# Layers 2 and 3 of a four-layer graph network written in source order, batch by batch

## The chip, the cores and the metric

The kernel runs on one core of a Trainium2 chip. The metric is the device time of one execution in microseconds (us), lower is better. A core has five engines with a queue of instructions each: PE (TensorE, matrix products; PEld is its weight load), DVE (VectorE), ACT (ScalarE), POOL (GpSimd) and SP (SyncE, which here only issues DMAs). Each engine takes its instructions in order; they wait for one another by semaphores.

## The reference, cut to what matters

x is (32, 512, 128): 32 batches of 512 nodes with 128 features; adj is one 512 x 512 matrix for all. Each of four layers normalises x, takes the ReLU as h, and adds the layer's output to x. The change touches layers 2 and 3:

```python
def layernorm(x): return (x - mean(x)) / sqrt(var(x) + 1e-5)      # over the features
# layer 2
h = maximum(layernorm(x), 0)
features = relu(h @ psi_w + psi_b)
messages = einsum('nm,bnd->bmd', adj * adj, features)
x = x + relu(concat(messages, h) @ phi1_w + phi1_b) @ phi2_w + phi2_b
# layer 3
h = maximum(layernorm(x), 0)
A = einsum('bnd,bmd->bnm', h @ q, h @ k) / sqrt(128)
A = exp(tanh(A / 8) * 8) * adj
x = x + (A / sum(A, -1)) @ h @ v
```

## The kernel before, in words

x stays in SBUF for all 32 batches, two batches to a group q (16 groups, `xt[q]`). Nodes are split into NT = 4 tiles of 128. Products that must be exact are made from fp32 operands of four-byte kind (f32, two PE instructions each) or from three `fp32r` parts of an operand, high, low and mid, with one PE instruction for each part and tile.

Three helpers make the parts. `moving_parts` (L397 to L399): high by a copy on ACT, low by a subtraction on POOL, mid by a scalar_tensor_tensor on DVE. `scaled_parts` (L403 to L405), for an operand that is LOW = 4096 times too large: high on ACT, low on DVE, then mid = high - low on POOL, which so waits for DVE. `fixed_parts` (L409 to L412) splits a weight.

**h and its transpose.** `stats_steps` (L243 to L254) has four bn_stats instructions for a group on DVE, a square root on ACT, a reciprocal and a product on DVE. `normed` (L263) makes h by eight ReLUs on ACT. `turn_steps` (L299 to L308) turns it feature-major: a 32 x 32 block transpose on DVE for each batch, four DMAs into a buffer in DRAM (d_hT), and one DMA back (hT, four buffers that layer 1 uses too).

**Layer 2, `layer2(q)`**, a generator for each group: h, hT; features (p_feat on PE, L1067 on DVE adds the bias, ReLU L1068 on ACT, `moving_parts`); messages (`mixed_parts`, L383, 12 matmuls for a batch with the three parts of the squared adj, evicted by ACT, L385); the bias phi2b added to x on POOL (L1081); the hidden layer (L1086, L1087, ReLU L1088 on ACT); the projection (p_l, L425) and the addition to x (L1092, DVE); then statistics for layer 3.

**Layer 3, `layer3(q)`**: h, hT; key parts by `moving_parts`; the product of the keys with qk = q k^T (L1116, three matmuls), evicted by DVE as qkh (L1118, scaled by LOW), and `scaled_parts` of it as the query; hv = h v with a column of ones (L1124, L1125); scores (L1131, 12 matmuls), Tanh (L1132) and Exp (L1136) on ACT, the mask product (L1138) for two tiles on DVE and two on POOL; A v (L1148, p_av, 32 instructions), a reciprocal (L1150) and an update of x (L1153, DVE); the store of the batch.

**What sets the order.** Layers 0 and 1 stand inside `tc.manual_schedule`, in which PE, DVE, ACT and POOL get their instructions in source order. It is left (`by_source.__exit__`, L1213) before layers 2 and 3. Their generators are stepped in turn (L1214 to L1223: `layer2` of groups 0 and 1, then one generator more in each turn), and the framework's scheduler, by its own costs and what is ready, then decides the order on each engine. Layer 1 calls `more(step)` around its last group: step 0 and 1 before the four blocks of `mix` (L977, L981), steps 2 to 5 after each.

Of the kernel before, what the change touches and what calls it, by code (L numbers as in the profile page):

```python
# [29 lines left out]
def kernel(  # L30
# [69 lines left out]
    def wide_tile(name, dtype=F32):  # L100
        return after.tile([P, 4, N], dtype, tag="wide", name=name, bufs=6)
# [92 lines left out]
    nc.vector.memset(eps, EPS)  # L194
    nc.scalar.activation(prep.tile([P, 1], F32, name="powers"), eps, AF.Exp)
# [14 lines left out]
    def ln_stats(q):  # L210
        for _ in stats_steps(q):
            pass
# [24 lines left out]
    def stats_steps(q):  # L237
# [11 lines left out]
        nc.scalar.activation(sd, st[:, :, :, 2], AF.Sqrt, bias=eps, scale=1.0 / D)  # L249
# [17 lines left out]
    def normed(q):  # L267
        h = normed_tile(q)
        for _ in normed_steps(q, h):
            pass  # L270
        return h
# [16 lines left out]
    def transposed(h, name):  # L288
        done = {}
        for _ in turn_steps(h, name, done):  # L290
            pass
        return done[name]
# [101 lines left out]

    def moving_parts(x, high, low, mid):

        nc.scalar.activation(high, x, AF.Copy, scale=DOWN)  # L397
        nc.gpsimd.tensor_sub(low, x, high.bitcast(F32))  # L398
        nc.vector.scalar_tensor_tensor(mid, x, 1.0 / UP, high.bitcast(F32), OP.mult, OP.subtract)  # L399
# [7 lines left out]
    def fixed_parts(x, high, low, mid):  # L407

        nc.scalar.activation(high, x, AF.Copy, scale=DOWN)  # L409
        nc.gpsimd.tensor_sub(x, x, high.bitcast(F32))  # L410
        nc.scalar.activation(low, x, AF.Copy, scale=LOW)
        nc.gpsimd.tensor_sub(mid, high.bitcast(F32), low.bitcast(F32))  # L412
# [635 lines left out]
    msgs, values, qk_parts = [], {}, []  # L1048

    def values_tile(q, b):  # L1050

        r = q + 2 * b
        if r not in values:
            values[r] = wide_tile(f"hv_{r}")
        return values[r].rearrange("p t n -> p (t n)").rearrange("p (b n) -> p b n", b=2)[:, b]

    def layer2(q):
        h = normed(q)
        yield
        hT = transposed(h, f"hT2_{q}")  # L1060
        yield
        yield
        feat = []
        for b in range(2):
            pf = projected(f"p_feat_{q}_{b}", (at(hT, b), psi))
            feat.append(small_tile(f"feat_{q}_{b}"))
            nc.vector.tensor_add(tiles(feat[b]), pf, spread(psib, NT))  # L1067
            nc.scalar.activation(feat[b], feat[b], AF.Relu)  # L1068
        right = [three(f"feat_{q}_{b}") for b in range(2)]
        for b in range(2):  # L1070
            moving_parts(feat[b], *right[b])
        yield
        if q % 2 == 0:
            msgs.append(wide_tile(f"msgT_{q}"))
        msgT = msgs[-1][:, 2 * (q % 2) : 2 * (q % 2) + 2]
        for b in range(2):
            mixed_parts(f"msgT_{q}_{b}", sq, right[b], msgT[:, b])
        for b in range(2):
            for i in range(0, NT, 2):
                xi = xt[q][:, b, i : i + 2, :]  # L1080
                tc.keep_in_program_order(nc.gpsimd.tensor_add(xi, xi, spread(phi2b, 2)))  # L1081
        yield
        h1T = msgT
        for b in range(2):
            ph = bank(f"p_phi1_{q}_{b}")
            nc.tensor.matmul(ph, phi1[:, 1, :], hT[:, :, b, :], start=True, stop=False)  # L1086
            nc.tensor.matmul(ph, phi1[:, 0, :], msgT[:, b], start=False, stop=True)  # L1087
            nc.scalar.activation(crossed(h1T[:, b]), split(ph), AF.Relu, bias=phi1b)  # L1088
        yield
        for b in range(2):  # L1090
            po = projected(f"p_l2_{q}_{b}", (columns(h1T[:, b]), phi2))
            nc.vector.tensor_add(xt[q][:, b], po, xt[q][:, b])  # L1092
        ln_stats(q)

    def layer3(q):
        h = normed(q)
        yield
        hT = transposed(h, f"hT3_{q}")
        yield
        keys = {}  # L1100

        def key_parts(b):
            both = wide_tile(f"key_{q}_{b}", F32R)
            keys[b] = [both[:, i].rearrange("p (t n) -> p t n", t=NQR) for i in range(3)]
            moving_parts(hT[:, :, b, :], *keys[b])

        if not qk_parts:
            parts = small_tile("qk_parts", F32R).rearrange("p (i f) -> p i f", f=D)
            qk_parts.extend(parts[:, i, :] for i in range(3))
            fixed_parts(qk, *qk_parts)  # L1110
        key_parts(0)
        yield
        for b in range(2):
            pp = bank(f"p_qkh_{q}_{b}")
            for i in range(3):
                nc.tensor.matmul(pp, qk_parts[i], keys[b][i], start=(i == 0), stop=(i == 2))  # L1116
            qkh = small_tile(f"qkh_{q}_{b}")
            nc.vector.tensor_scalar(crossed(qkh), split(pp), UP * LOW, None, OP.mult)  # L1118
            query = three(f"query_{q}_{b}")
            scaled_parts(qkh, *query)  # L1120

            pv = projected(f"p_hv_{q}_{b}", (at(hT, b), vw))
            hv = values_tile(q, b)[:, : NT * (D + 1)].rearrange("p (t f) -> p t f", f=D + 1)
            nc.vector.memset(hv[:, :, D : D + 1], 1.0)  # L1124
            nc.vector.tensor_copy(hv[:, :, :D], pv)  # L1125
            yield
            ex = wide_tile(f"ex_{q}_{b}")
            for t in range(NT):
                ps = bank(f"p_score_{q}_{b}_{t}")
                for i in range(3):  # L1130
                    nc.tensor.matmul(ps, keys[b][i][:, t, :], query[i], start=(i == 0), stop=(i == 2))  # L1131
                nc.scalar.activation(ex[:, t, :], ps, AF.Tanh, scale=UP / (8.0 * math.sqrt(D)))  # L1132
            if b == 0:
                key_parts(1)
            for t in range(NT):
                nc.scalar.activation(ex[:, t, :], ex[:, t, :], AF.Exp, scale=8.0)  # L1136
                eng = nc.gpsimd if t % 2 and q + b > 0 else nc.vector
                eng.tensor_mul(split(ex[:, t, :]), split(ex[:, t, :]), crossed(adjTx[0][:, t, :]))  # L1138
            yield
            out_r = out[2 * q + b].rearrange("(t p) f -> p t f", p=P)  # L1140
            rsum = stats.tile([P, NT], F32, tag="rsum", name=f"rsum_{q}_{b}", bufs=4)
            final = b == 1 and q == NQ - 1
            n = 1 if final else 2
            for i0 in range(0, NT, n):
                po = bank(f"p_av_{q}_{b}_{i0}").rearrange("p (i f) -> p i f", i=2)[:, :n]
                for i in range(n):
                    for t in range(NT):
                        nc.tensor.matmul(po[:, i, : D + 1], ex[:, t, blk(i0 + i)], hv[:, t, :],  # L1148
                                         start=(t == 0), stop=(t == NT - 1))
                nc.vector.reciprocal(rsum[:, i0 : i0 + n], po[:, :, D])  # L1150
                for i in range(n):
                    xi = xt[q][:, b, i0 + i, :]
                    nc.vector.scalar_tensor_tensor(xi, po[:, i, :D], rsum[:, i0 + i : i0 + i + 1], xi,  # L1153
                                                   OP.mult, OP.add)
                if final:
                    nc.sync.dma_start(out_r[:, i0, :], xt[q][:, b, i0, :])
            if not final:
                nc.sync.dma_start(out_r, xt[q][:, b])
# [22 lines left out]
    def load_mask():  # L1181

        yield
        adjTx.append(matrix_tile("adjTx"))
        load_crossed(adjTx[0], adjT_d)

    second = [layer2(q) for q in range(NQ)]
    made_square = square()

    def more(step):  # L1190

        if step in (0, 1):
            next(second[0])
        elif step == 2:
            next(second[0])
            next(second[1])
        elif step == 3:
            next(second[1])
        elif step == 5:
            ln_stats(NQ - 2)  # L1200
            ln_stats(NQ - 1)
# [10 lines left out]
    go(made_square)  # L1212
    by_source.__exit__(None, None, None)  # L1213
    waiting = [second[:2]] + [[second[q]] for q in range(2, NQ)]  # L1214
    waiting[-2].append(load_mask())
    waiting += [[layer3(q)] for q in range(NQ)]
    active = []
    while waiting or active:
        if waiting:
            active += waiting.pop(0)  # L1220
        if not waiting and len(active) == 2:
            active.reverse()
        active = [g for g in active if next(g, active) is not active]  # L1223
# [32 lines left out]
```

## Time and profile before

| what | value |
|---|---|
| median of the 3 runs shown | 936.29 us (934.6 to 937.66) |
| profiled execution, its own time | 934.17 us |
| span of it, first to last instruction | 932.1 us |
| granted PE clock over the span | 0.996 |
| first feature product of layer 2 starts | 457.5 us |
| first message product of layer 2 starts | 462.0 us |
| first score of layer 3 starts | 664.9 us |
| A v of the last batch, last start | 928.7 us |

The times of single instructions come from the profiled execution, which took 934.17 us, 2.1 us more than its span and 2.1 us less than the median of the runs. A window's row gives its length, then for each engine the busy time and the number of instructions, then the granted PE clock, the share of the DMA engines and GB/s. A group's row gives the engine, the operation, what is written and read, the number, busy time and mean of one in ns, and the idle time of its engine before it with what ended it. A row of the waits gives total us, how often, and the longest.

### The profile page before, as it was taken

What the parts mean: (1) busy time and instruction counts of PE and PEld (TensorE: products, weight loads), DVE (VectorE), ACT (ScalarE), POOL (GpSimd) and SP (SyncE); (2) the same over time, 40 slices, a digit from 0 to 9 for tenths busy, and PEclk for the clock granted to TensorE, in tenths of its full rate; (3) what the DMA queues carried; (4) which work ended last, traced back from release to release, by engine and by line L of the source; (5) the groups of instructions that cost most, each with busy time, mean ns of one, the idle gap of its engine ahead of it and who ended that gap; (6) DMA issues with size and microseconds to landing.
All of it is one profiled execution on the core that took longest, in us unless ns stands there. A gap on an engine that the chain in (4) does not pass through costs nothing.

```text
span 932.1 us, 15187 instructions
## 1 busy us (share of the span) xinstructions
PE 908.0 (97%) x5433; PEld 777.9 (83%) x5433; DVE 693.7 (74%) x1318; ACT 547.6 (59%) x1192; POOL 530.3 (57%) x461
## 2 busy tenths in 40 slices
PE   8999999999999999999899999999999999999997
PEld 4899999878888888888777777777779999999996
DVE  8888885665665655565754676767799999999995
ACT  5864552342452352353877778777767675757573
POOL 5868999742132253532135555447358787777874
PEclk9999999999999999999999999999999999999999
DMA  9256643113213312302443434343322221212111
GB/s 256 61 165 176 172 119 100 46 46 91 66 40 112 85 39 68 91 24 68 114 136 108 119 106 130 99 142 112 114 86 74 71 65 61 76 58 80 34 35 46
DMA packets 83914, 86.05 MB, mean 92 GB/s; under 512 B 6784, under 2 KB 74624, under 8 KB 83840
## 3 DMA queue, kind: packets, MB, share of 16 engines
q1 hardware_dynamic: 83552, 84.57, 31.8%
q8 instruction: 43, 0.70, 0.3%
q10 hardware_dynamic: 288, 0.52, 0.2%
q14 instruction: 31, 0.25, 0.1%
HBM read 44.17 MB, written 40.89 MB: 91 GB/s over the span
## 4 chain that ended last, share of the span: by engine, by line
PE 87%; ACT 5%; DVE 4%; POOL 2%; issue 1%; DMA 0%; POOLq 0%; ACTq 0%; DVEq 0%
PE p_av L1148 11%; PE p_l L981 10%; PE p_msgT L383 9%; PE p_score L1131 8%; PE p_x1T L383 7%; PE p_w L425 5%; PE p_l_c L371 4%; PE p_l L977 3%; PE p_l_a L371 3%; PE p_l_d L371 3%; PE p_phi L1086 3%; PE p_phi L1087 3%; PE p_g L425 3%; PE p_l L425 3%; PE p_hv L425 3%; PE p_feat L425 3%
## 5 line engine op out<-in xcount | busy, mean ns | idle before, releaser
L263 ACT ACTIVATE h<-x,sh,rs 128x128 f32<-128x128 f32 x512 | 208.2, 483 | 18.1 <-DVE sh L252 13.1
L1148 PE MATMUL p_av<-hv,ex 128*128 128x129 f32 x1024 | 122.7, 277 | 4.8 <-DVE ex L1138 3.7
L1148 PEld LDWEIGHTS p_av<-hv,ex 128*128 128x128 f32 x1024 | 120.3, 193 | 7.6 <-DVE ex L1138 4.5
L398 POOL TENSOR_TENSOR low_feat<-feat,high_feat 128x512 fp32r<-128x512 f32 x32 | 52.3, 1650 | 119.5 <-ACT high_feat L397 111.5
L1138 POOL TENSOR_TENSOR ex<-ex,adjTx 128x512 f32<-128x512 f32 x62 | 98.8, 1614 | 34.7 <-ACT ex L1136 33.5
L398 POOL TENSOR_TENSOR low_h<-h,high_h 128x512 fp32r<-128x512 f32 x32 | 48.5, 1523 | 78.6 <-ACT high_h L397 78.3
L1132 ACT ACTIVATE ex<-p_score 128x512 f32<-128x512 f32 x128 | 66.3, 612 | 44.6 <-PE p_av L1148 38.9
L385 ACT ACTIVATE x1T<-p_x1T 128x512 f32<-128x512 f32 x32 | 18.9, 592 | 124.3 <-POOL low_h L398 74.4
L243 DVE BATCH_NORM_STATS2 bn<-x 128x6 f32<-128x256 f32 x248 | 88.4, 416 | 0.2
L299 DVE STREAM_TRANSPOSE hb_hT<-h 128x512 f32<-128x512 f32 x120 | 80.1, 688 | 4.8 <-DMA d_hT<-hb_hT 2.1
L1138 DVE TENSOR_TENSOR ex<-ex,adjTx 128x512 f32<-128x512 f32 x66 | 72.3, 1101 | 13.0 <-ACT ex L1136 11.6
L1136 ACT ACTIVATE ex<-ex 128x512 f32<-128x512 f32 x128 | 71.3, 662 | 0.1
L952 POOL COPY hs<-hT 128x512 f32<-128x512 f32 x32 | 18.7, 615 | 83.7 <-DMA hT<-d_hT 82.7
L398 POOL TENSOR_TENSOR key<-hT,key 128x512 fp32r<-128x512 f32 x32 | 55.4, 1746 | 17.7 <-ACT key L397 16.9
L249 ACT ACTIVATE sd<-bn,eps 128x8 f32<-128x8 f32 x62 | 18.8, 303 | 72.0 <-DVE bn L243 67.8
L405 POOL TENSOR_TENSOR mid_query<-high_query,low_query 128x512 fp32r<-128x512 f32 x32 | 41.7, 1302 | 27.9 <-DVE low_query L404 14.1
L983 DVE SCALAR_TENSOR_TENSOR p_l<-p_l,b 128x512 f32<-128x512 f32 x32 | 22.4, 700 | 46.0 <-PE p_l L981 46.0
L1067 DVE TENSOR_TENSOR feat<-p_feat,psib 128x512 f32<-128x512 f32 x32 | 21.8, 684 | 44.1 <-PE p_feat L425 44.0
L1131 PE MATMUL p_score<-high_query,key 128*128 128x512 f32 x128 | 52.9, 417 | 0.8 <-ACT high_query L403 0.8
L425 PE MATMUL p_w<-th,x1T 128*128 128x128 f32 x256 | 50.3, 278 | 3.2 <-ACT x1T L385 3.2
L1131 PE MATMUL p_score<-mid_query,key 128*128 128x512 f32 x128 | 50.3, 394 | 0.5 <-POOL mid_query L405 0.4
L1131 PE MATMUL p_score<-low_query,key 128*128 128x512 f32 x128 | 49.7, 390 | 0.0
(212 smaller groups left out, 2373.1 us busy)
## 6 DMA issues: line engine op xcount, KB each, us to landing
d_hT<-hb_hT SPq DMA_DIRECT2D x240, 128.0 KB, 2.5
hT<-d_hT SPq DMA_DIRECT2D x60, 512.0 KB, 3.5
x<-in_x_dram SPq DMA_DIRECT2D x32, 256.0 KB, 5.8
out_dram<-x SPq DMA_DIRECT2D x31, 256.0 KB, 2.4
adjT_d<-adj_squares SPq DMA_DIRECT2D x4, 256.0 KB
adj_crossed<-in_adj_dram SPq DMA_DIRECT2D x4, 256.0 KB
adjTx<-adjT_d SPq DMA_DIRECT2D x4, 256.0 KB
adj_s<-in_adj_dram ACTq DMA_DIRECT2D x2, 256.0 KB, 3.8
```

The lines of the kernel that those rows point to most:

```text
L243: nc.vector.bn_stats(st[:, k].rearrange("p e s -> p (e s)"), xt[q][:, b, t : t + 2, :].rearrange("p t f -> p f t"))
L263: nc.scalar.activation(h[:, b, t, :], xt[q][:, b, t, :], AF.Relu, bias=shift[q][:, i : i + 1], scale=scale[q][:, i : i + 1])
L299: nc.vector.transpose(hb[:, :, b].rearrange("p j t r -> p t j r"), h[:, b].rearrange("p t (j c) -> p t j c", c=QR))
L371: nc.tensor.matmul(p[:, i * 2 * D : (i + 1) * 2 * D], a[:, k, blk(i)], b[:, k], start=(first and i == 0 and k == 0), stop=(k == 1), skip_g ...
L383: nc.tensor.matmul(p, right[part][:, blk(t)], left[part][:, t, :], start=(t == 0 and part == 0), stop=(t == NT - 1 and part == 2))
L398: nc.gpsimd.tensor_sub(low, x, high.bitcast(F32))
L425: nc.tensor.matmul(p[:, blk(t)], hT(t), w, start=(i == 0), stop=(i == len(terms) - 1))
L981: nc.tensor.matmul(p, adj_parts[part][:, t, blk(i)], w[r][part][:, t, :], start=False, stop=(part == 2 and t == NT - 1), skip_group_check= ...
L1131: nc.tensor.matmul(ps, keys[b][i][:, t, :], query[i], start=(i == 0), stop=(i == 2))
L1136: nc.scalar.activation(ex[:, t, :], ex[:, t, :], AF.Exp, scale=8.0)
L1138: eng.tensor_mul(split(ex[:, t, :]), split(ex[:, t, :]), crossed(adjTx[0][:, t, :]))
L1148: nc.tensor.matmul(po[:, i, : D + 1], ex[:, t, blk(i0 + i)], hv[:, t, :], start=(t == 0), stop=(t == NT - 1))
```

## The change

Everything up to the end of the kernel stays in source order: `by_source.__exit__` comes after layers 2 and 3, which are now one function, `layers_2_and_3`. It has two loops over the 32 batches, and each loop writes steps of several batches.

- **Layer 2's loop**, for batch n: `messages(n)`; `chunk` (h of batch n + 6); eviction of the messages, now on DVE; `biased(n)`; `features(n + 2)`; `hidden(n - 1)`; `updated(n - 2)`, with statistics for layer 3 after each second batch; in 20 places also `chunk(3, m)`, the normalisation of a batch m for layer 3; then `turn_half`, the DVE transposes of these chunks and, with each second one, the four DMAs to DRAM.
- Turned h of layer 3 stays in DRAM (a buffer for each group) until `fetch` reads it, up to four groups ahead of its use.
- Layer 3's statistics are made with eps and variance scaled (`low=True`), so that h of layer 3 is LOW times as large. So the keys are split by `scaled_parts` (ACT, DVE, POOL) in place of `moving_parts`, and vw is divided by LOW once.
- The queries are split straight from PSUM by a new `bank_parts`: high on ACT, low and mid on DVE; qkh and POOL's share are gone.
- **Layer 3's loop**, for batch n: `queries(n + 1)`, `scores(n)` (Exp of a tile after the next tile's Tanh), `attended(n - 1)`, `mapped(n + 1)` (hv), `key_parts(n + 2)`, in 12 batches a chunk and a transpose for later batches, and `fetch` in each second batch.
- `more` now also makes features of batches 0 and 1 between the last blocks of layer 1, and h of batches 0 to 5.

Cut to its core:

```diff
+    def bank_parts(p, high, low, mid):
+        nc.scalar.activation(high, p, AF.Copy, scale=UP * DOWN)
+        nc.vector.scalar_tensor_tensor(low, p, UP, high.bitcast(F32), OP.mult, OP.subtract)
+        nc.vector.tensor_sub(mid, p, high.bitcast(F32))
...
+    def features(n):
...
+        hT = hT_of(2, n)
+        pf = projected(f"p_feat_{n}", (lambda t: hT[:, t, :], psi))
+        feat = small_tile(f"feat_{n}")
+        nc.vector.tensor_add(tiles(feat), pf, spread(psib, NT))
+        nc.scalar.activation(feat, feat, AF.Relu)
+        feats[n] = three(f"feat_{n}")
+        moving_parts(feat, *feats[n])
...
+    def key_parts(n):
...
+        both = wide_tile(f"key_{n}", F32R)
+        keys[n] = [both[:, i].rearrange("p (t n) -> p t n", t=NQR) for i in range(3)]
+        scaled_parts(hT_of(3, n), *keys[n])
+
+    def queries(n):
...
+        p = bank(f"p_query_{n}")
+        for i in range(3):
+            nc.tensor.matmul(p, qk_parts[i], keys[n][i].rearrange("p b (a c) -> p a b c", c=QR),
+                             start=(i == 0), stop=(i == 2))
+        query[n] = three(f"query_{n}")
+        bank_parts(p, *query[n])
+
+    def mapped(n):
...
+        p = projected(f"p_hv_{n}", (lambda t: hT[:, t, :], vw))
+        hv = hvs[n] = after.tile([P, NT, D + 1], F32, tag="small", name=f"hv_{n}", bufs=13)
+        nc.vector.memset(hv[:, :, D : D + 1], 1.0)
+        nc.vector.tensor_copy(hv[:, :, :D], p)
...
+        for n in range(B):
+            p = messages(n)
+            ready = []
+            if n + 6 < B:
+                chunk(2, n + 6)
+                ready.append((2, n + 6))
+            elif n % 2:
+                ready.append((3, ahead_of_3()))
+            nc.vector.tensor_scalar(msgT[n // 4][:, n % 4], p, UP, None, OP.mult)
+            biased(n)
+            features(n + 2)
+            hidden(n - 1)
+            updated(n - 2)
+            if n > 8 and n % 3 or n + 6 >= B:
+                ready.append((3, ahead_of_3()))
+            for layer, m in ready:
+                turn_half(layer, m)
...
+        for n in range(B):
+            queries(n + 1)
+            scores(n)
+            attended(n - 1)
+            mapped(n + 1)
+            key_parts(n + 2)
+            if n % 4 != 3:
+                m = ahead_of_3()
+                if m is not None:
+                    turn_half(3, m)
+            if n % 2 == 0:
+                fetch(3, n // 2 + 3)
+        attended(B - 1, 1)
...
     next(next_layer)
     go(made_square)
+    layers_2_and_3()
     by_source.__exit__(None, None, None)
-    waiting = [second[:2]] + [[second[q]] for q in range(2, NQ)]
-    waiting[-2].append(load_mask())
-    waiting += [[layer3(q)] for q in range(NQ)]
-    active = []
-    while waiting or active:
...
```

## The prediction

> **What bounds the kernel now.** I read the page's engine totals first, then the 20 us windows, then one batch of layer 3 in the timeline, and last the waits of PE. Totals and windows (us; busy and count of PE, PEld, DVE, ACT, POOL; granted clock; DMA share; GB/s):
>
> ```profile
> PE 908.0 (97%) x5433; PEld 777.9 (83%) x5433; DVE 693.7 (74%) x1318; ACT 547.6 (59%) x1192; POOL 530.3 (57%) x461
> ```
> ```profile
> 480.00:500.00 20.00, 17.28 (x88) 13.35 (x87) 11.99 (x25) 12.49 (x29) 6.20 (x6) 0.91 0.37 106
> 580.00:600.00 20.00, 20.00 (x114) 16.36 (x113) 11.59 (x22) 16.92 (x40) 6.81 (x7) 1.00 0.43 126
> 680.00:700.00 20.00, 18.00 (x97) 15.31 (x96) 18.25 (x33) 15.04 (x30) 11.80 (x8) 0.91 0.36 105
> 740.00:760.00 20.00, 20.00 (x144) 18.54 (x143) 19.37 (x39) 12.42 (x25) 15.56 (x10) 1.00 0.21 66
> 860.00:880.00 20.00, 20.00 (x141) 18.40 (x140) 19.37 (x34) 13.25 (x26) 16.49 (x11) 1.00 0.09 27
> ```
>
> PE never rests in layers 2 and 3 except near 460, 490, 670 to 690 and 918 us; DVE is close behind it in layer 3 (19.4 of 20). A full PE need not be at its peak, so the timeline (start, duration):
>
> ```profile
> 743.52 0.47 PE L1131 MATMUL p_score<-high_query,key 128*128 128x512 f32 x1
> 743.84 0.39 PE L1131 MATMUL p_score<-low_query,key 128*128 128x512 f32 x1
> ...
> 746.37 0.84 PE L1116 MATMUL p_qkh<-key,qk_parts 128*128 128x512 f32 x3
> 747.05 1.05 PE L425 MATMUL p_hv<-vw,hT 128*128 128x128 f32 x8
> 747.94 3.74 PE L1148 MATMUL p_av<-hv,ex 128*128 128x129 f32 x32
> 751.43 0.48 PE L1131 MATMUL p_score<-high_query,key 128*128 128x512 f32 x1
> ```
>
> Start to start: 12 score matmuls take 2.85 us, 3 query matmuls 0.68, 8 p_hv 0.89, 32 p_av 3.49: 7.9 a batch. The ten windows from 700 to 900 hold 1418 matmuls, 55 to a batch: 25.8 batches, 7.76 us each. So layer 3 runs at PE's issue rate now. Layer 2 does too: 32 matmuls a batch (12 x 0.23 + 16 x 0.11 + 4 x 0.43 = 6.2 us), and 114 in the 20 us from 580 are 5.6 us each. What an order can still win is PE's rest:
>
> ```profile
> PE p_msgT L383 <- ACT high_feat L397: 4.5, 2, 2.5
> PE p_av L1148 <- DVE ex L1138: 3.7, 3, 1.5
> ```
>
> With the smaller rests near these times it is 2.7 + 2.7 + 4.2 + 1.2 = 10.8 us, and two half-clock stretches of 3.4 us cost 1.7 each: **at most 15 us.**
>
> **The change, layer 2.** PE's matmuls are the same in number and size. On DVE the eviction of p_msgT comes in (ACT's 0.58 becomes a DVE row like L1118's, 0.68). As built, one batch on DVE is, in order: evict 0.68, add of L1067 0.68, a wait for ACT's ReLU and high copy (0.62 + 0.63 and two hops of 0.08: 1.4), mid split 1.05 (mean of L399), add of L1092 0.68, one transpose 0.69: 5.2 us. Each second batch adds statistics: four of L243 (1.41 together), 0.54 until ACT's square root is there, 0.35. That is 6.4 us a batch against PE's 6.2. Twenty of layer 3's transposes are moved in here (0.67 each); ACT has room for their normalisations (4 x 0.42, on some 3.7 us a batch). DVE's sum: 32 x 6.4 + 20 x 0.67 less what the last batches don't have (6 transposes, 2 feature steps) = 208 us; PE's is 197. DVE may fall some 7 us behind before PE waits, since features are made two batches ahead, so the difference comes out where layer 3 starts. At the start, p_feat of batches 0 and 1 moves ahead of L981's last two blocks; its hT can land at about 452 to 454 (d_hT writes issued from 445.6, 4.1 to landing each way), PE comes to it at 449.7, so what is saved at 460 is given back: first p_msgT at 462, as now. Sum: 462 + 208, then key split, queries and updates of the last batches, 7 us: **first score at 677** (664.9 now, there overlapped with the rest of layer 2). Bounds: 666 if only PE counts, 688 if ACT's added work stalls DVE by 0.35 a batch. SP issues the same DMAs; layer 3's writes and fetches stand three or more batches ahead of use, hT's four buffers and hb's two come free before SP or DVE gets to them, so I cost them at nothing; where that cover fails, one landing, 4 us.
>
> **The change, layer 3: the step that decides.** The loop writes queries(n+1), scores(n), attended(n-1), mapped(n+1), key_parts(n+2). All engines keep that order, so PE's last work of a round is p_hv of n+1 and the first of the next is p_query of n+2. The latter needs key_parts(n+2): its low part is a DVE instruction that stands right behind the copy of p_hv(n+1), its mid part is POOL's and needs low. Behind p_hv there is thus a chain that nothing on PE covers, because scores, p_av and p_hv are queued behind the waiting p_query. Its rows (line, forms, count, busy, mean ns, idle before):
>
> ```profile
> L1125 DVE COPY hv<-p_hv 128x512 f32<-128x512 f32 x32 | 21.7, 679 | 0.1
> L404 DVE SCALAR_TENSOR_TENSOR low_query<-high_query,qkh 128x512 fp32r<-128x512 f32 x32 | 47.8, 1493 | 0.2
> L405 POOL TENSOR_TENSOR mid_query<-high_query,low_query 128x512 fp32r<-128x512 f32 x32 | 41.7, 1302 | 27.9 <-DVE low_query L404 14.1 <-DVE rsum L1150 9.0 <-PE p_qkh L1116 4.8
> ```
>
> These are the very operations (split with LOW: DVE low, POOL mid) that now serve the queries. L404 ranges from 677 to 1766 ns, the short ones where POOL rests; in the new order POOL's two mask products are over by then, so I take 0.68, and 1.28 for mid (its median). Count from the third query matmul: that 0.23, scores 2.85, p_av 3.49, p_hv 0.89, its end 0.2 later: 7.7. Hop 0.1, copy 0.68, low 0.68, hop 0.08, mid 1.28, hop 0.09: **10.6 us.** The other way round the ring is as long: high query on ACT at 0.5 to 1.1, four Tanh and Exp interleaved from 1.25 (0.52 and 0.56 each), third Exp over at 5.3, mask product on DVE to 6.3 (1.1), four updates and two reciprocals 1.6 (L1153, L1150), then copy, low, mid: 10.8. I take 10.7 against 7.76. That bank_parts takes the L1118 eviction (21.7 us) and 26 us of L404 off DVE, adds 21.7 for mid, and frees POOL of 41.7, wins nothing while this chain stands. The query matmuls now read their keys in runs of 32 elements; L1086, which reads hT in runs of 128, takes 592 ns like L1087, which reads straight on, so I cost that at nothing (at the other end twice the 0.23 of a matmul, of which only the third lies outside the pause: 0.2 a round).
>
> **The clock.** Windows of 3.41 us, laid so that one begins where the clock fell:
>
> ```profile
> 460.98:464.39 3.41, 2.17 (x8) 1.51 (x9) 3.41 (x8) 2.33 (x5) 2.32 (x2) 1.00 0.43 149
> ...
> 488.29:491.70 3.41, 1.19 (x4) 0.67 (x4) 3.35 (x8) 2.84 (x6) 1.67 (x1) 1.00 0.00 0
> 491.70:495.11 3.41, 3.29 (x8) 2.63 (x9) 1.82 (x3) 1.23 (x4) 3.41 (x5) 0.50 0.82 178
> ...
> 686.29:689.70 3.41, 1.45 (x8) 0.83 (x7) 3.41 (x3) 3.41 (x9) 3.41 (x3) 1.00 0.58 145
> 689.70:693.11 3.41, 3.41 (x16) 3.27 (x16) 3.41 (x3) 1.60 (x5) 3.41 (x3) 0.50 0.00 0
> ```
>
> A window in which PE worked 1.19 or 1.45 us is followed by one at half clock; with 2.17, and with 1.99 in the window before, nothing happened. The new pause of 7.5 to 10.7 us holds only the first two query matmuls, some 2.4 us of rest, so a window laid at chance over it falls under the limit in about two of three rounds. The half-clock stretch then lies on the next scores: the last Tanh starts 0.8 to 1.6 us later. Two thirds of 1.2 is **0.8 us a round**; bounds 0 and 1.6. Round: 11.5 us.
>
> The Trainium skill's "TensorE: Matmul & The Clock Gate" (section "HAM oscillation — how this bites in real kernels") gives the rule as no idle gaps above some 3.4 us. By it the split pause would leave the clock alone and the sum would be 1018; the rows above show the fall at gaps of 2.05 and 0.67.
>
> **Sum, against the profiled execution** (span 932.1, time 934.17; the median shown, 936.29, is 2.1 above it). First score 677; to the second round's query 9.4 (no p_av yet); 29 rounds of 11.5, 333.5; then scores 30, p_av 29, scores 31, p_av 30, masks and p_av of 31, last update and store: 19. 1038.9, and 2.1 outside the span: 1041. **Forecast 1040 us.**
>
> **Rivals.** (1) The same pause at full clock: rounds of 10.7, 677 + 9.4 + 310 + 19 + 2.1 = 1018. For it: after 1.99 and 2.17 us of work nothing fell. Chance 0.28; mine 0.55. (2) The chain is dearer: low at L404's 1.5, mid at 1.74 (L398's median beside DVE work; twelve rounds have a transpose there), and every round cold, 1.6: rounds of 13.6 at most, 13 where not all coincide: 1085. 0.09. (3) The other side: the key parts are ready before PE has done p_hv, so no pause. Then only the 15 us of rests go, 919. It decides where the pause is under 0.5 us a round (15 us over 30); DVE would have to reach low before the copy of p_hv, which its order forbids. 0.06. Within 0.3% of 936, what a measurement of this kernel can't tell from no change: 0.02, a pause of half a microsecond. Faster by more 0.06, slower by more 0.92.
>
> **Range.** Low: first score 666, rounds of 10.5: 666 + 9.4 + 304.5 + 19 + 2.1 = 1001, and some 8 lower if the copy's hops are shorter. High: 688 and 12.3: 688 + 9.4 + 356.7 + 19 + 2.1 = 1075, and part of (2). 993 to 1080.
>
> **What would show it.** PE busy in layer 3 near 70%; PE's largest wait p_query for POOL's key, about 30 times some 1 us, and for DVE's key, 30 times 1.4; 5 to 5.5 batches in 60 us; granted clock under 1 in many windows, mean 0.85 to 0.95 there; in layer 2 PE waits of a few us in all, first score near 677. It is wrong if p_query's waits are absent or if POOL and DVE do key parts before p_hv.

## The result, and the profile after

The changed kernel takes **1035.09 us** (median of 4 runs, 1034.23 to 1035.74) against 935.75 before on the same chip: ratio 1.1059, 95% interval 1.1037 to 1.108, slower. The forecast was 1040 us, its range 993 to 1080. The profiled execution took 1035.37 us, its span is 1033.4, its mean granted clock 0.976 (0.996 before).

Engine totals of the changed kernel, from its page (busy us, share of the span, instructions):

```profile
PE 940.0 (91%) x5433; PEld 789.3 (76%) x5433; DVE 645.1 (62%) x1350; ACT 535.5 (52%) x1157; POOL 466.0 (45%) x431
```

PE has the same 5433 matmuls. DVE and POOL have 49 and 64 us less to do and the kernel is 99 us longer: no engine has become the bound, so look for waits. PE's largest waits (engine, operation, line, what ended the wait: us in all, times, longest):

```profile
PE p_query L1154 <- DVE key L410: 34.4, 31, 1.1
PE p_query L1154 <- POOL key L411: 27.8, 31, 0.9
PE p_feat L430 <- DMA hT<-d: 10.3, 3, 4.2
PE p_query L1154 <- ACT key L409: 7.5, 2, 4.6
```

Two waits in each of 31 rounds, 62 us, both of p_query for parts of its key; then three of p_feat for an hT on its way through DRAM. One round on PE (start, duration; in brackets the idle time before and what ended it):

```profile
818.14 0.50 PE L1154 MATMUL p_query<-key,qk_parts 128*128 128x512 f32 x1 [0.90 <-POOL key L411]
818.48 0.39 PE L1182 MATMUL p_score<-high_query,key 128*128 128x512 f32 x1
...
821.28 3.73 PE L1200 MATMUL p_av<-hv,ex 128*128 128x129 f32 x32
824.85 1.06 PE L430 MATMUL p_hv<-vw,hT 128*128 128x128 f32 x8
825.66 0.48 PE L1154 MATMUL p_query<-key,qk_parts 128*128 128x512 f32 x1
827.28 0.50 PE L1154 MATMUL p_query<-key,qk_parts 128*128 128x512 f32 x1 [1.15 <-DVE key L410]
828.70 0.51 PE L1154 MATMUL p_query<-key,qk_parts 128*128 128x512 f32 x1 [0.91 <-POOL key L411]
```

And what DVE and POOL do in the same pause:

```profile
825.94 0.69 DVE L1167 COPY hv<-p_hv 128x512 f32<-128x512 f32 x1
826.55 0.68 DVE L410 SCALAR_TENSOR_TENSOR key<-key,hT 128x512 fp32r<-128x512 f32 x1
```
```profile
827.37 1.27 POOL L411 TENSOR_TENSOR key<-key 128x512 fp32r<-128x512 f32 x1 [2.08 <-DVE key L410]
```

Read them as one chain: p_hv ends, its copy, key low, key mid, third query matmul. From third query to third query the round is 10.56 us; the kernel before does a batch in 7.91 (two p_hv starts two batches apart: 778.69 and 794.51). The same windows as before (busy and count of PE, PEld, DVE, ACT, POOL; clock; DMA):

```profile
480.00:500.00 20.00, 20.00 (x102) 15.34 (x101) 13.69 (x22) 11.26 (x25) 9.91 (x10) 1.00 0.28 80
580.00:600.00 20.00, 20.00 (x102) 15.34 (x101) 14.02 (x30) 13.71 (x32) 9.38 (x10) 1.00 0.39 106
620.00:640.00 20.00, 16.69 (x72) 12.19 (x72) 13.94 (x29) 11.50 (x26) 9.50 (x9) 0.83 0.37 106
680.00:700.00 20.00, 13.72 (x57) 11.38 (x58) 11.53 (x22) 10.04 (x19) 4.96 (x4) 0.76 0.19 60
740.00:760.00 20.00, 17.04 (x101) 14.52 (x102) 10.04 (x22) 13.03 (x26) 7.35 (x6) 0.91 0.24 76
860.00:880.00 20.00, 17.65 (x109) 15.41 (x109) 9.71 (x23) 10.94 (x20) 6.82 (x6) 0.91 0.14 39
```

Between its stalls layer 2 keeps PE full, with DVE at only 14 of 20. Layer 3 holds about 105 matmuls in 20 us where it held 140.

By stage, measured against the prediction's terms: first score 685.7 (677); to the second round's third query 697.1, 11.4 (9.4); 29 rounds to 1011.0, 313.9 or 10.83 each (333.5, 11.5 each); from there to the end 22.4 (19). The sum is 5.5 us under the prediction's 1041, because the rounds were overstated by 19.6 and the rest understated by 14.1. That the total came so close is thus in part luck: two errors of opposite sign.

### The profile page after: what moved, and what is told of

Read it like the earlier page. It is cut to its first block, busy times and chain, and to the rows that moved or that the text cites. A ratio compares the mean times of both kernels' runs of the same rounds, so it can differ in the third digit from the quotient of the medians.

```text
span 1033.4 us, 15149 instructions
## 1 busy us (share of the span) xinstructions
PE 940.0 (91%) x5433; PEld 789.3 (76%) x5433; DVE 645.1 (62%) x1350; ACT 535.5 (52%) x1157; POOL 466.0 (45%) x431
## 5 line engine op out<-in xcount | busy, mean ns | idle before, releaser
L1177 POOL TENSOR_TENSOR ex<-ex,adjTx 128x512 f32<-128x512 f32 x64 | 87.6, 1368 | 155.9 <-issue 131.7
L404 POOL TENSOR_TENSOR low_feat<-feat,high_feat 128x512 fp32r<-128x512 f32 x32 | 55.9, 1746 | 134.6 <-ACT high_feat L403 134.6
L1154 PE MATMUL p_query<-key,qk_parts 128*128 128x512 f32 x96 | 48.3, 506 | 69.7 <-DVE key L410 34.4
L1177 DVE TENSOR_TENSOR ex<-ex,adjTx 128x512 f32<-128x512 f32 x64 | 50.6, 791 | 70.5 <-ACT ex L1175 70.5
L415 ACT ACTIVATE high_query<-p_query 128x512 fp32r<-128x512 f32 x32 | 19.2, 599 | 135.1 <-PE p_query L1154 135.1
L1154 PEld LDWEIGHTS p_query<-key,qk_parts 128*128 128x128 f32 x96 | 18.4, 192 | 90.8 <-DVE key L410 44.3
L1183 ACT ACTIVATE ex<-p_score 128x512 f32<-128x512 f32 x128 | 76.3, 597 | 14.4 <-PE p_score L1182 10.9
L404 POOL TENSOR_TENSOR low_h<-h,high_h 128x512 fp32r<-128x512 f32 x32 | 48.3, 1515 | 78.4 <-ACT high_h L403 78.1
L1175 ACT ACTIVATE ex<-ex 128x512 f32<-128x512 f32 x128 | 77.0, 630 | 0.0
L411 POOL TENSOR_TENSOR key<-key 128x512 fp32r<-128x512 f32 x32 | 40.8, 1277 | 75.4 <-DVE key L410 75.4
L416 DVE SCALAR_TENSOR_TENSOR low_query<-p_query,high_query 128x512 fp32r<-128x512 f32 x32 | 22.1, 692 | 74.5 <-ACT high_query L415 74.4
L405 DVE SCALAR_TENSOR_TENSOR mid_feat<-feat,high_feat 128x512 fp32r<-128x512 f32 x32 | 25.2, 789 | 45.8 <-ACT high_feat L403 45.8
```

The source lines that it names most:

```text
L1154: nc.tensor.matmul(p, qk_parts[i], keys[n][i].rearrange("p b (a c) -> p a b c", c=QR), start=(i == 0), stop=(i == 2))
L1183: nc.scalar.activation(ex[:, t, :], p, AF.Tanh, scale=UP / (8.0 * math.sqrt(D)))
```

## The experiments

**Theory**: the chain behind p_hv lengthens each round; clock and the way through layer 2 are additions. **Rivals**: the lost time lies in the turned-h traffic or in p_query's own reads; or the clock carries it; or the other ring (ACT and DVE) would hold the round anyway.

**1. Keys one round earlier.** key_parts(2) is written ahead of the loop, and each round makes the parts for three batches ahead.

```
+        key_parts(2)
         for n in range(B):
...
-            key_parts(n + 2)
+            key_parts(n + 3)
```

> The changed kernel with the key parts of layer 3 made one round earlier: key_parts(n + 3) in place of n + 2 at the end of a round, key_parts(2) ahead of the loop. No instruction is added or left out. Theory 1 (the pause is the chain p_hv, copy of hv, low part on DVE, mid part on POOL, p_query): p_query finds its parts ready, the 1.15 and 0.91 us waits of 30 rounds go, and with them the second of the three matmuls' start; a round falls from 10.55 to PE's own 7.8 us, 30 x 2.8 = 84 us less, and some 6 us of half clock: 940 to 950 us. Theory 2 (the other way round the ring, ACT's Tanh and Exp and DVE's mask products and updates, is the bound, and the wait at p_query only shows it): the order of DVE and ACT is the same, so a round stays above 10 us: 1020 or more.

Measured: **945.98 us** (ratio to before 1.0105, 1.008 to 1.013): 89 us of the 99 are gone. One window of layer 3:

```profile
800.00:820.00 20.00, 20.00 (x149) 18.65 (x148) 14.21 (x34) 15.09 (x30) 10.70 (x8) 1.00 0.26 80
```

PE is full at full clock, a round is 7.95 us (queries at 700.88 and 923.53, 28 rounds). Layer 3's DRAM traffic and the reads in runs of 32 are still there, so neither costs its rounds more than 0.04 us a batch against the 7.91 before. No ring through ACT and DVE holds the round either, at least not above 7.95.

**2. Queries one place later.** Instead, the keys stay where they are and queries(n + 1) is written behind scores(n).

```
         for n in range(B):
-            queries(n + 1)
             scores(n)
+            queries(n + 1)
             attended(n - 1)
```

> The changed kernel with one line moved: queries(n + 1) behind scores(n) instead of ahead of it. Theory 1: the chain behind p_hv (3.1 us) now runs beside the 2.85 us of the next scores, so 0.2 to 0.5 us of the pause is left at p_query; but the split of the query in ACT then stands behind the Exps of the same round, and low and mid behind the mask products, some 8 us after the round began, so the next scores may wait up to 0.5 us: rounds of 8 to 8.6, 950 to 970 us. Theory 2 (ACT and DVE ring): a round stays above 10, 1020 or more.

Measured: **949.69 us** (1.0144, 1.0115 to 1.0172), at the lower end of theory 1, with rounds of 7.99. Once the scores have begun PE waits for no p_query, only once for ACT's high query, 4.1 us ahead of the second batch's scores. Moving one call by one place covers the chain with 2.8 us of score matmuls. So it isn't where the keys are made that costs, but that nothing on PE lies between p_hv and the query that waits.

**3. The pause filled.** Eight 128x512 matmuls into the query's bank stand ahead of each query from batch 2 on; the query then overwrites them.

```
+        if n > 1:
+            for _ in range(8):
+                nc.tensor.matmul(p, keys[n - 1][0][:, 0, :], keys[n - 1][0], start=True, stop=True)
```

> The changed kernel with eight more matmuls of 128 x 512 ahead of each batch's p_query from batch 2 on; they write into the query's bank, which the first real matmul then overwrites, so they only use PE: 8 x 0.23 = 1.8 us a round, 55 us in all. Theory 1 (PE waits for a chain that doesn't depend on PE): they run in the pause (1.15 us and more before the low part is there) and cost 0 to 0.5 us a round in time, while the clock no longer falls in layer 3: between 1025 and 1045 us. If PE's own rate set the round, they would cost all: 1090. The clock: the five half-clock stretches of layer 3, which lengthen a round by 1.5 us each, go: granted clock 1.0 from 705 us on.

Measured: **1027.54 us** (1.097, 1.0941 to 1.0999). PE has 240 matmuls more, 55 us at 0.23 each, and is 7.5 us faster. Rounds are 10.54 (third queries at 803.24, 813.77, 824.33), as the rounds at full clock were, and from batch 3 on none is longer: granted clock 1.00 in the windows from 740 to the end. PE still waits for the end of the chain in every round:

```profile
PE p_query L1157 <- POOL key L411: 15.9, 31, 1.2
```

So the chain alone sets the round. Of the 8.8 us between the spans of the two profiled executions, 1.7 lie ahead of the first score (684.02 and 685.69), where the kernels are the same; the half clock of layer 3 cost the other 7 (5.4 in the 29 rounds, 1.6 behind them).

**4. Keys ahead of the copy.** key_parts(n + 2) is written before mapped(n + 1), which takes only the copy of hv out of the chain.

```
             attended(n - 1)
+            key_parts(n + 2)
             mapped(n + 1)
-            key_parts(n + 2)
```

> The changed kernel with two lines exchanged: key_parts(n + 2) ahead of mapped(n + 1) in a round. On DVE the low part of the keys then stands ahead of the copy of hv and no longer waits for p_hv; PE's order is the same. Theory 1: one link of the chain, the copy of 0.69 us, goes; the low part starts when the updates of x are over (0.8 us behind the last p_av), so a round falls by 0.6 to 0.7 us: 30 rounds, 18 to 21 us, 1013 to 1018 us. Theory 2 (the wait is for p_hv itself, not for what stands behind it): the whole pause would go, 945. Theory 3 (DVE's load): same instructions, no change, 1033 to 1037.

Measured: **1004.64 us** (1.0727, 1.0697 to 1.0758). The round is 9.78 (third queries at 805.07 and 814.85), 0.78 shorter; in 30 rounds 23 us. That is theory 1, but the time lies below its 1013 to 1018. Some 6 of the other 7 us are the clock, which the expectation had left out: from batch 3 on every round is 9.76 to 9.81, none at half clock; experiment 3 gives much the same size for that. The rest, 1.5 us in the profiled executions, lies ahead of the first score (684.15 and 685.69). In PE's waits the link that is left is now first:

```profile
PE p_query L1154 <- POOL key L411: 26.4, 29, 0.9
PE p_query L1154 <- DVE hv L1166: 11.0, 29, 0.4
```

The "hv" here is the memset beside the copy, the next DVE instruction after key low; the profile names the last signal of the queue, not the operation that p_query needs.

**5. The mask later.** The load of adjTx moves in layer 2 of the changed kernel from batch 20 to batch 29.

```
-            if n == 20:
+            if n == 29:
                 adjTx.append(matrix_tile("adjTx"))
                 load_crossed(adjTx[0], adjT_d)
```

> The changed kernel, only the load of the mask (adjTx, 1 MB) moved from batch 20 to batch 29 of layer 2. Theory: of the three waits of p_feat for hT that delay layer 3, the one at 623.8 us (3.3 us, then half clock, some 1.7 us more) comes from this load, which is pushed ahead of the writes of d; without it p_feat does not wait there, the first score comes at 680 to 681 instead of 685.7, and the time is 1030 (1028 to 1032). Rival: the wait comes from layer 3's own writes and fetches crowding the queue, and the load has nothing to do with it: the wait stays, time 1035 (1033 to 1037).

Measured: **1028.92 us** (1.0972, 1.0943 to 1.1), 6.2 us less, within what the theory expected. The wait near 620 us is gone, with the 6.8 us at half clock (3.4 us lost) behind it, and the first score comes at 678.80 instead of 685.69. Two of the three waits for hT are left in experiment 5:

```profile
PE p_feat L430 <- DMA hT<-d: 6.9, 2, 4.0
```

The changed kernel's DMA issues on SP's queue and DVE's transposes show how the load reached PE:

```profile
602.78 1.75 SPq L1078 DMA_DIRECT2D d<-hb  x4
604.58 2.62 SPq L116 DMA_DIRECT2D adjTx<-adjT_d  x4
609.35 3.21 SPq L1078 DMA_DIRECT2D d<-hb  x4
620.38 0.34 SPq L1085 DMA_DIRECT2D hT<-d  x1
```
```profile
620.43 0.71 DVE L1073 STREAM_TRANSPOSE hb<-h 128x512 f32<-128x512 f32 x1 [6.60 <-DMA d<-hb]
```

The writes of d that share the time with this 1 MB land late (the last, issued at 611.96, at 620.31, where the median write takes 2.4 us); the two hb buffers serve both layers' transposes, so the next transpose waits 6.6 us for one, the fetch of hT behind it is issued at 620.4, and p_feat, due at 620.5, waits until 623.8 and then runs at half clock.

**6. Against the stalls of layer 2, on experiment 1.** The mask at batch 29; the second pair's transpose and fetch ahead of p_feat of batch 0; p_feat of batches 0 and 1 each one block of layer 1 later; keys of batches 0 and 1 made during batches 29 and 30.

```
             chunk(2, 3)
-            features(0)
             turn_half(2, 3)
             fetch(2, 1)
         elif step == 4:
             chunk(2, 4)
-            features(1)
+            features(0)
             turn_half(2, 4)
         elif step == 5:
+            features(1)
...
+            if n in (29, 30):
+                key_parts(n - 29)
-        key_parts(0)
-        key_parts(1)
```

> The kernel with keys three batches ahead (946.0 us), and with its stalls in layer 2 mended: the mask loaded at batch 29 instead of 20; turn_half and fetch of the second pair written ahead of p_feat of batch 0, and p_feat of batches 0 and 1 each one block of layer 1 later; the keys of batches 0 and 1 split during batches 29 and 30. Theory: the waits of 3.0, 4.0, 3.3 and 4.0 us and their half-clock stretches (1.7 to 2.5 us each) go, some 20 us: 926 (922 to 932), below the kernel before (935.8). If it holds, what the new order can win is PE's rest, once its waits are off PE's path. Rival: PE's waits turn up in other places (feature parts too late for the first p_msgT, keys behind the chunks on ACT): 938 to 946.

Measured: **931.23 us** (930.89 to 931.47; before 937.22 in 13 runs on that chip; ratio 0.9929, 0.9909 to 0.9949): a version faster than both kernels, by 0.5 to 0.9% over the one before. It is at the upper end of the theory's range, and PE still waits in and around layer 2:

```profile
PE p_feat L430 <- DMA hT<-d: 3.5, 1, 3.5
PE p_w L430 <- ACT x1T L390: 1.7, 1, 1.7
PE p_phi L1121 <- DVE msgT L1239: 1.4, 1, 1.4
```

The first hT is fetched only at 452.41, because two of the next pair's writes of d now come ahead of it on SP's queue, and PE reaches p_feat at 453.0.

**7. The query copied out of its bank again, on experiment 1.** This undoes the part "queries split from the bank" and the turned reads of the keys.

```
-            nc.tensor.matmul(p, qk_parts[i], keys[n][i].rearrange("p b (a c) -> p a b c", c=QR),
+            nc.tensor.matmul(p, qk_parts[i], keys[n][i],
                              start=(i == 0), stop=(i == 2))
...
-        bank_parts(p, *query[n])
+        qkh = small_tile(f"qkh_{n}")
+        nc.vector.tensor_scalar(crossed(qkh), split(p), UP, None, OP.mult)
+        moving_parts(qkh, *query[n])
```

> The kernel with keys three batches ahead (946.0 us), but the queries go the way of the kernel before: p_query from keys read straight on, copied out of the bank on DVE (turned on the way), then split in high, low and mid on ACT, POOL and DVE. Theory: with the chain off PE's path the split straight from the bank is worth nothing, because the parts are needed only a round later and POOL has room (1.28 us more a batch on 10 of 20): 946 (944 to 949). Rival 1: the way of the queries through four engines in place of three lies on the path of the first scores or of each round: over 950. Rival 2: reading keys in runs of 32 cost something (up to 0.2 us a round): 940 or less.

Measured: **966.24 us** (1.0304, 1.0281 to 1.0326): rival 1, and the theory fell. Part of one ring of experiment 7, on DVE and then on ACT:

```profile
827.61 0.68 DVE L1169 COPY hv<-p_hv 128x512 f32<-128x512 f32 x1
...
828.21 0.68 DVE L410 SCALAR_TENSOR_TENSOR key<-key,hT 128x512 fp32r<-128x512 f32 x1
828.81 0.68 DVE L1158 TENSOR_SCALAR qkh<-p_query 128x512 f32<-128x512 f32 x1
```
```profile
829.59 0.63 ACT L403 ACTIVATE high_query<-qkh 128x512 fp32r<-128x512 f32 x1 [3.22 <-DVE qkh L1158]
830.12 1.06 ACT L1185 ACTIVATE ex<-p_score 128x512 f32<-128x512 f32 x2
...
837.99 0.63 ACT L403 ACTIVATE high_query<-qkh 128x512 fp32r<-128x512 f32 x1 [3.23 <-DVE qkh L1158]
```

ACT's high query waits for DVE's copy out of the bank; that stands behind key low and the hv copy, these behind p_av's updates and DVE's mask product, and that behind the Exps, which ACT does only after high query. The ring takes 8.40 us in these lines against 7.95, and 9.0 in the rounds in which DVE does a transpose as well (0.6). With the split straight from the bank, high query needs nothing of DVE and there is no ring. So this part of the change is worth 20 us once the key chain is away. While that chain holds the round at 10.56, a ring of 9.0 should be hidden under it; no run has the copied query together with the chain.

**8. Less of layer 3 made ready during layer 2, on experiment 1.** 13 instead of 20 normalisations and transposes.

```
-            if n > 8 and n % 3 or n + 6 >= B:
+            if n > 19 and n % 3 or n + 6 >= B:
                 ready.append((3, ahead_of_3()))
...
-            if n % 4 != 3:
-                m = ahead_of_3()
-                if m is not None:
-                    turn_half(3, m)
+            m = ahead_of_3()
+            if m is not None:
+                turn_half(3, m)
```

> The kernel with keys three batches ahead (946.0 us), with 13 instead of 20 of layer 3's normalisations and transposes done during layer 2, the other 19 one in each round of layer 3. Theory: neither layer is bound by DVE or ACT (13 to 14 of 20 us busy in layer 2, 14 to 17 in layer 3), so the place of this work decides nothing: 946 (944 to 949). Rival (the prediction's own term, DVE behind PE in layer 2): the seven transposes taken out of layer 2 (0.67 each, 4.7 us) bring the first score forward by 4 to 5 us, to 682, and the time to 941 to 942.

Measured: **937.93 us** (1.0008, 0.9991 to 1.0024), 8 us under experiment 1, more than either expected. It isn't DVE's work: the first score comes at 678.32 instead of 687.10, and in experiment 5, with all 20 transposes in place, at 678.80. What is absent, as in experiment 5, is the wait for hT at 620 us, and the transposes' longest wait for hb is 2.85 us where experiment 1's was 6.47. It makes 6.4 of the 8.8 us between the first scores: the message products of batch 24 start 3.0 us earlier than in experiment 1, those of batch 25 9.3 us. The 3 us are there from batch 2 on, where the two kernels are still the same, and the batches between, with fewer transposes, add nothing to them. Fewer transposes of layer 3 beside the mask means that hb is free in time. Experiments 5 and 8 take away the same stall from its two sides, so it needs both the load and the extra turns.

## Why the prediction was right or wrong

- **The chain in layer 3: right in mechanism and size.** "Round, 10.7" was 10.56 at full clock, its PE way summed to 10.6. Members: copy 0.69 (0.68), low 0.68 (0.68), mid 1.27 (1.28). Experiments 1, 2 and 4 each take out a different part of it, and the time follows.
- **"The clock +0.8 a round": the step that was mis-sized.** 10.83 less 10.56 is 0.27 a round. "About two of three rounds" was five of 29 (12.09 to 12.52 each), the first of them still from the waits at the start of layer 3. The rows were read rightly, the odds weren't: I laid the 3.41 us windows at chance, but in these traces they keep a fixed pace, and so do the rounds. The clock halved at 742.42, 807.27, 872.12 and 936.97: each time 64.85 us on, which is 19 windows and six rounds, one of them 12.1 long. Windows on that pace:

```profile
803.85:807.26 3.41, 1.71 (x6) 1.22 (x7) 1.40 (x4) 0.60 (x1) 1.26 (x1) 1.00 0.79 231
933.56:936.97 3.41, 1.79 (x7) 1.26 (x8) 0.78 (x3) 0.61 (x2) 1.26 (x1) 1.00 0.81 230
936.98:940.39 3.41, 3.41 (x10) 2.63 (x9) 1.85 (x3) 2.81 (x5) 0.00 (x0) 0.50 0.01 3
998.41:1001.82 3.41, 1.82 (x7) 1.28 (x8) 0.78 (x3) 0.63 (x2) 1.26 (x1) 1.00 0.27 79
1001.83:1005.24 3.41, 3.41 (x24) 3.06 (x23) 1.82 (x3) 3.36 (x7) 0.55 (x1) 1.00 0.02 5
687.80:691.21 3.41, 1.72 (x12) 1.40 (x10) 1.67 (x5) 3.38 (x6) 0.00 (x0) 1.00 0.19 64
```

  With 1.79 us of PE work in a window laid over the pause the clock halves, with 1.82 it doesn't. In other stages the busy time alone doesn't decide: the window with 1.72 us at 687.80 stays without a fall, as does one with 1.53 in experiment 3 (at 622.06). PE rests 2.06 us in the pause (1.15 and 0.91), not the 2.4 I took, so a window must take in all but some 0.45 us of both rests. Laid at chance, about half of the rounds would have one (an estimate: the pause is 2.6 us from end to end, so 1.7 of 3.41 us of positions do). That only five of 29 had one is the pace: a round of 10.54 us is three windows and 0.30 us, one with a fall, 12.09, three and 1.85. By this count a fall moves the pauses behind it out of reach, and five rounds of 0.30 us bring them back. Experiment 4 leaves 1.29 us of rest: at least 2.1 us of work in the windows laid over it, and no fall. With no half clock from batch 3 on, rival (1), the kernel takes 1028 (experiment 3).
- **The rule of the Trainium skill** ("TensorE: Matmul & The Clock Gate", section "HAM oscillation — how this bites in real kernels"), that PE should have no idle gaps above some 3.4 us, is not enough here: the clock also fell in rounds whose longest gap is 1.15 us. The sum by it, 1018, is 17 us under the measured time, some 7 of which are half clock in layer 3.
- **"Layer 2 bound by DVE, 6.4 a batch": wrong in the mechanism.** DVE had 14 of 20 us to do and PE no rest between stalls. Added to DVE, layer 3's transposes cost nothing as work (first score 678.80 with 20 of them in experiment 5, 678.32 with 13 in experiment 8). The row that misled is L399's mid split, 1.05 us on average before; in the new order it takes mostly 0.69 (mean of the new line L405: 0.79). The sum itself slips a little too: 5.2 and half of the 2.3 for statistics are 6.3, not 6.4, some 2 us in 32 batches.
- **"SP and DMAs at nothing; where the cover fails, 4 us": the cover failed three times.** p_feat waited 2.8 us at 452, 4.2 at 470 and 3.3 at 624, each followed by half clock. The first was foreseen (first p_msgT 462, measured 463.0). The second, as the trace shows it, comes from the order on SP's queue, which is not among the four engines that keep source order:

```profile
457.50 8.06 SPq L1078 DMA_DIRECT2D d<-hb  x5
465.74 0.34 SPq L1085 DMA_DIRECT2D hT<-d  x1
```

  The four writes of the second pair had landed at 461.2, but its fetch stands behind a write of the third pair, which waited for a transpose until 465.2. In experiment 6, with that transpose and fetch written earlier, this wait is gone. For the third wait, "hT's four buffers and hb's two come free before SP or DVE gets to them" was the failing step: hb didn't, behind the mask's load, which I hadn't put on SP's queue beside the writes.
- **First score 677, measured 685.7.** Without the 620 us stall it is 678.8 (experiment 5), near the forecast, but from two errors that cancel: 11 us of DVE work behind PE that weren't there, and, about as long, the wait at 470 with its half clock and the 2.9 and 0.9 us for which p_query of batch 0 waits for its key, which were.
- **"Second round's query 9.4 later": 11.4.** p_query waits 4.6 us for ACT's key high, which stands behind a table load of 1.28 us and the first batch's Tanh and Exp. **Tail 19: 22.4**: half clock over the scores of batch 30 (1.5 to 1.7 us) and a p_hv of 0.8 that I left out make some 2.4 of it; the last 1 us is not followed up.
- **bank_parts "wins nothing while this chain stands": right** as far as it was tested: with bank_parts and the chain the round was the forecast chain's, and the copied query's ring of 9.0 us lies under it, but no run has that copy beside the chain. Experiment 7 shows what bank_parts wins without the chain. **p_query in runs of 32 at nothing: right** (at most 0.04 a batch). **7.76 us a batch before** was 2% low: the rounds read from p_hv to p_hv are 7.91. Windows count a matmul on their border twice; 1397 start between 700 and 900, not 1418.
- **"At most 15 us" to win:** experiment 6 wins 6 (0.7%), with some 9 us of waits left.

## What to carry to other kernels

When each engine runs its queue in the order of the source, walk once round the loop and ask at each place where PE passes from its last work of a round to the next round's first: what must other engines do between the two, and what stands on PE in that time? If the answer is "three instructions" and "nothing", the loop pays their sum every round, here 2.6 us of 10.6, though DVE, ACT and POOL are half idle; making the operand a round earlier, or putting one covered block in between, takes nearly all of it back (rounds of 7.95 and 7.99). Buffers that two streams share couple the streams: look at which transfer frees each before you call a transfer hidden.

## What the runs showed of the hardware

- The clock followed windows of 3.41 us at a fixed pace, and over the pause of this loop it halved with up to 1.79 us of PE work in one and not with 1.82; elsewhere 1.53 and 1.72 us went by without a fall, so busy time alone is no limit. The loop loses clock only when its phase and the windows' agree, here once in six rounds; the cost is a beat, not an average over chance positions. 55 us of matmuls put into the pause made the kernel 7.5 us faster.
- The same instruction took very different times: DVE's mask product 1.10 us on average before and 0.79 after, POOL's 1.61 and 1.37, DVE's mid split 1.05 and 0.79. On DVE it goes with POOL's work: in the kernel before, the low split of the query (L404) took 0.68 to 0.69 us in the five cases without a POOL instruction beside it and 1.51 to 1.77 in the other 27, while the copy out of the bank (L1125) took 0.68 either way. Such a row's mean from a stage with a busy POOL overstates the operation where POOL rests.
